# Moving the look for negative elements of adj from layer 0 to layer 3, and lists, ranks and descriptions ahead of layer 0's last additions

## The chip, the core and the metric

The kernel runs on one core of a Trainium2 chip. Its engines work side by side, each through its own queue in program order: TensorE (PE, with its weight loads PEld), VectorE (DVE), ScalarE (ACT), GpSimd (POOL) and SyncE (SP), which here only issues DMA transfers; ACT issues some too. The metric is the device time of one execution in microseconds.

## The reference

There is a table x of 2708 rows of 128 numbers and a weighted adjacency matrix adj of 2708 x 2708, of which some 0.6% and the diagonal are nonzero. Four layers each add a term to x, computed from h = max(layernorm(x), 0):

- Layer 0: x += (adj^T h) / column sums of adj.
- Layer 1: messages gelu(s_i + d_j + b) for every pair (i, j), weighted with adj[i, j] and summed over j; then an update with a gelu, a layernorm and a residual. s and d are h times two 128 x 128 matrices.
- Layer 2: agg = adj h, a matrix with a relu, and a GRU cell on it and h.
- Layer 3: graph attention with two heads, softmax over the neighbours (adj > 0, or the diagonal), a layernorm, a matrix and an elu for each head, and their mean.

## The kernel before

x, h and small tables stay in SBUF. Rows are taken in 22 tiles of 128 (the last has 20 rows), four tiles make a group (six groups, the last of two tiles), columns are taken in 22 blocks of 124.

**Layer 0** reads adj once, in cuts c = 0 to 5 of four column tiles, and in each cut the row groups s = 0 to 5. `load_cut` brings one piece of 512 rows x some 560 columns into a ring of four buffers `a` (DMA from SP); the pieces of the narrow cut 5 go to tiles `z` of their own. For each piece, `list_cut` finds on DVE the eight largest values of each row in each block of 124 columns with their positions (`val`, `col`), because layer 1 works on lists of the nonzero elements. `work_cut` turns the piece's blocks on PE (L409), copies them out of PSUM on ACT to `aT` (L413), stores them as adjT in DRAM (DMA from ACT, L363), and multiplies the piece into the sums (L384, PE). `look` (L395, ACT) passes over half a piece at a time with Relu(-a) and an accumulated sum in `below`; a sum above zero later makes the kernel take its dense path, since lists of the largest values don't hold negative elements. Small steps of the layernorms (`spread`, `sum_rows`, `sum_squares`, `normal_rows`) go between these on ACT.

The order of the work here is written out by hand: under `manual_schedule` every engine executes in the order of the program text. Cut 5's pieces are worked within cut 4; their lists are made later, in `list_last`.

**Hand-over.** After the last `work_cut` come `list_last(0)`, counts of row entries (`count_some`), `add(LAST)` (the last group's sums added to x, `invert` at L446), further lists, `rank(0)` (a matmul with a triangular matrix, L590, whose result goes to `ends` and, spread fourfold, to `ends4`, L591 and L592), the moments of x, lists 4 to 16, `add(LAST - 1)`. A second list of steps inside layer 1 then selects, describes and places the entries of the first tiles: `describe` splits the values of one tile into three bf16 parts with column numbers and ends (ACT, DVE, POOL); `select_rows` compares on DVE (L657) and shifts the result by one row with two DMAs from SP (`later`); `finish_rows` subtracts (L731); `fetch` multiplies on PE (L742); `place` picks each entry's value and column; `pass_on` spreads column numbers through DRAM; `columns` compares them.

**Layer 1** then runs in 22 periods, one tile each, with PE full. **Layer 2** reads adjT in chunks of 512 columns, and writes a byte `mask` of the nonzero elements. **Layer 3** goes through the row tiles in runs of 3, 8, 8 and 3: for each source tile and head, `weigh` makes weights on DVE (L1139) and PE multiplies them into sums (L1169). Between runs `evacuate` empties the PSUM banks by ACT and DVE (L1215), and `close` finishes two tiles at a time: moments on DVE, scaling on ACT (L136), turning on PE (L1243), a copy on ACT (`z4T`, L1246), matmuls (L1252), the elu on ACT, and the store of `y` (DMA from SP). These steps are generators that `follow` registers; `advance` takes the next step of each when a modelled clock, counted up by `spend`, has passed the units that the step yielded. At the end a `flag` with all reasons for the dense path is summed by a matmul and read by the engines.

Of the kernel before, what the change touches and what calls it, by code (L numbers as in the profile page):

```python
# [20 lines left out]
F32 = mybir.dt.float32  # L21
# [9 lines left out]
P = 128  # L31
# [29 lines left out]
def listed_layers(ctx: ExitStack, tc: tile.TileContext, x, adj, w, out, flag):  # L61
# [99 lines left out]
    below = keep.tile([P, 2 * len(GROUPS) ** 2], F32, name="below")  # L161
    nc.gpsimd.memset(below, 0.0)
# [129 lines left out]
    turned = l0.enter_context(tc.tile_pool(name="l0t", bufs=10))  # L292
# [72 lines left out]
    def work_cut(c, s, between=()):  # L365
# [23 lines left out]
        e0, e1 = t0 * P - lo, t0 * P - lo + span(t0, tk)[1]  # L389

        def look(half):
            q0, q1, m = (2 * half, 2 * half + 2, P) if gk == 4 else (half, half + 1, size(g0 + half))
            junk = pool.tile([P, 2, CH], U8, name="junk0", bufs=1)
            i = 2 * (len(GROUPS) * c + s) + half
            nc.scalar.activation(  # L395
                junk[0:m, 0 : q1 - q0, 0 : e1 - e0], a[0:m, q0:q1, e0:e1], AF.Relu, scale=-1.0,
                accum_out=below[0:m, i : i + 1],
            )

# [3 lines left out]
        for js in turns:  # L403
# [16 lines left out]
            turn_of = [t for t, v in enumerate(turns) if v is js][0]  # L420
            if len(turns) == 2 or turn_of % 2 == 1:
                look(turn_of * 2 // len(turns))
# [166 lines left out]
    def rank(t, p):  # L589
        nc.tensor.matmul(p[:, 0:NB], before, rows_n[:, t, :], start=True, stop=True)  # L590
        nc.vector.tensor_copy(ends[:, t, :], p[:, 0:NB])  # L591
        nc.vector.tensor_copy(ends4, p[:, 0:NB].unsqueeze(2).to_broadcast([P, NB, R]))  # L592
# [3 lines left out]
    add(LAST)  # L596
# [3 lines left out]
    rank(0, bank("p_r"))  # L600
    measure(LAST)
    for n in range(4, 17):
        list_last(n)
# [27 lines left out]
    with (  # L631
# [9 lines left out]
        def split(dst, src, rest):  # L641

            nc.scalar.copy(dst[0], src)
            nc.vector.tensor_tensor(rest, src, dst[0], ALU.subtract)
            nc.scalar.copy(dst[1], rest)
            nc.gpsimd.tensor_tensor(dst[2], rest, dst[1], ALU.subtract)

# [65 lines left out]
        def describe(t):  # L713
            x = xb[t % 2]
            rest = once.tile([P, NB, S], F32, name="v_r")
            split([x[:, :, q * S : (q + 1) * S] for q in range(3)], val[:, t, :, :], rest)
            nc.gpsimd.tensor_copy(x[:, :, 3 * S : 4 * S], col[:, t, :, :])
            nc.gpsimd.tensor_copy(x[:, :, C - 1], ends[:, t, :])
# [1204 lines left out]
```

## Time and profile before

| | |
|---|---|
| median of 3 runs | 1057.58 us (1057.03, 1057.58, 1063.91) |
| profiled execution, time | 1063.71 us |
| profiled execution, span | 1061.9 us |
| granted clock of PE, mean | 0.943 |
| PE busy | 934.5 us (88%) |
| PE weight loads busy | 817.3 us (77%) |
| DVE busy | 797.8 us (75%) |
| ACT busy | 518.4 us (49%) |
| POOL busy | 471.1 us (44%) |

In the trace's time the layers lie about so: layer 0 from 0 to 231 us, the hand-over to 287, layer 1 to 610, layer 2 to 777, layer 3 to the end. A row of a group has the line, the engine and operation, the tiles written and read with their shapes, how often, busy time and mean duration, and the engine's idle time just before with what ended it. A row of the timeline begins with the start and the duration in us; brackets hold the idle time before it and what ended that. A row of waits says who waited for whom: total us, times, longest. The share of an engine over the whole span is a mean of stages with different limits, so stretches of the span are read by themselves.

### The profile page before, as it was taken

The page shows a single profiled execution, that of the slowest core. Times are in us where ns is not written, and L with a number is a line of the kernel's source. Part 1 is how long each engine was busy: PE and PEld are TensorE (multiplying, and loading weights), DVE is VectorE, ACT ScalarE, POOL GpSimd, SP SyncE. Part 2 cuts the span into 40 slices and gives each one's busy share as a digit, 9 for nine tenths or more (in the row PEclk, how much of TensorE's full clock was granted, in tenths as well). Part 3 has the DMA queues.
Part 4 walks back from the last instruction along what each step waited for, and adds up shares of the span by engine and source line. Part 5 has one row for each costly group of instructions (what it writes and reads, how often), then busy time and mean ns, then how long its engine had stood idle before and what let it go on. Part 6 is the DMA issues. An engine that isn't in the chain of part 4 may idle for free. (4 is left out here: it accounts for less than half of the span.)

```text
span 1061.9 us, 23359 instructions
## 1 busy us (share of the span) xinstructions
PE 934.5 (88%) x8632; PEld 817.3 (77%) x8632; DVE 797.8 (75%) x2754; ACT 518.4 (49%) x1471; POOL 471.1 (44%) x589
## 2 busy tenths in 40 slices
PE   6799788972499999999999969999979999989983
PEld 5699688751499999999899824444568899989982
DVE  7999797747677878887868264656578977997793
ACT  6887678752466666667666521433322200330142
POOL 6222222312597778898979173344311300250042
PEclk9999898975699999999999979999989999999996
DMA  9799799521234343233322065556410000000000
GB/s 299 244 316 363 231 362 358 187 68 58 79 125 125 99 125 121 96 105 113 101 95 83 12 223 186 199 188 221 129 35 21 12 4 1 2 16 6 1 15 15
DMA packets 77091, 133.65 MB, mean 126 GB/s; under 512 B 13980, under 2 KB 29456, under 8 KB 76966
## 3 DMA queue, kind: packets, MB, share of 16 engines
q1 hardware_dynamic: 56986, 99.92, 29.0%
q10 hardware_dynamic: 19980, 32.14, 8.4%
q8 instruction: 70, 1.15, 0.5%
q14 instruction: 55, 0.45, 0.1%
HBM read 85.41 MB, written 30.87 MB: 109 GB/s over the span
## 5 line engine op out<-in xcount | busy, mean ns | idle before, releaser
L787 POOL TENSOR_SCALAR put<-count,line,value 128x128 f32<-128x128 f32 x176 | 204.5, 1176 | 37.0 <-DVE value L776 36.9
L1169 PE MATMUL att<-hv,wt 128*128 128x129 f32 x1672 | 195.4, 277 | 8.8 <-DVE wt L1139 7.3
L1169 PEld LDWEIGHTS att<-hv,wt 128*128 128x128 f32 x1672 | 191.8, 194 | 11.8 <-DVE wt L1139 7.0
L869 PE MATMUL p_m<-s,sel 128*128 128x128 bf16 x1452 | 162.7, 221 | 6.0 <-ACT g L881 5.8
L873 PE MATMUL p_m<-d,cols 124*128 124x128 bf16 (+1 forms) x1452 | 163.0, 221 | 0.7 <-DVE cols L818 0.7
L1139 DVE SCALAR_TENSOR_TENSOR wt<-row,lift,mask 128x1024 f32<-128x1024 f32 (+1 forms) x132 | 138.0, 1075 | 24.6 <-PE att L1169 24.5
L120 POOL TENSOR_TENSOR n_r<-n_r,minus_half 128x4 f32<-128x4 f32 (+1 forms) x28 | 39.9, 1425 | 236.2 <-DVE n_r L119 232.3
L384 PE MATMUL sums<-h,a 128*128 128x129 f32 (+1 forms) x880 | 124.5, 291 | 1.5 <-ACT h L136 1.5
L894 PE MATMUL agg<-put,g 128*128 128x128 f32 (+1 forms) x968 | 122.5, 278 | 0.0
L1308 PE MATMUL p_agg<-a,hs 128*128 128x512 f32 (+2 forms) x264 | 111.2, 564 | 12.2 <-issue 6.2
L384 PEld LDWEIGHTS sums<-h,a 128*128 128x128 f32 (+1 forms) x880 | 115.1, 206 | 2.8 <-issue 2.3
L894 PEld LDWEIGHTS agg<-put,g 128*128 128x128 f32 x968 | 113.1, 192 | 0.0
L869 PEld LDWEIGHTS <-sel 128*128 128x128 bf16 x1452 | 104.3, 98 | 7.5 <-issue 7.0
L873 PEld LDWEIGHTS <-cols 124*128 124x128 bf16 (+1 forms) x1452 | 103.5, 98 | 1.0 <-DVE cols L818 1.0
L409 PE MATMUL p_T<-ident,a 128*128 128x128 f32 (+1 forms) x440 | 75.4, 292 | 29.4 <-ACT aT L413 23.0
L796 ACT ACTIVATE put<-mine,value 128x128 f32<-128x128 bf16 x308 | 100.6, 392 | 0.0
L881 ACT ACTIVATE g<-p_m 128x512 f32<-128x512 f32 x132 | 72.7, 552 | 54.9 <-PE agg L894 41.2
L1308 PEld LDWEIGHTS p_agg<-a,hs 128*128 128x128 f32 (+1 forms) x264 | 48.3, 197 | 61.5 <-issue 53.6
L357 DVE FIND_INDEX8 col<-val,a 128x8 uint16<-128x124 f32 x342 | 91.7, 279 | 0.0
L355 DVE MAX8 val<-a 128x8 f32<-128x124 f32 x342 | 79.2, 273 | 13.0 <-DMA a<-in_adj 13.0
L409 PEld LDWEIGHTS p_T<-ident,a 128*128 128x128 f32 (+1 forms) x440 | 54.4, 149 | 40.5 <-ACT aT L413 28.4
L413 ACT COPY aT<-p_T 128x512 f32<-128x512 f32 (+2 forms) x122 | 67.9, 560 | 17.8 <-PE p_T L409 17.3
(271 smaller groups left out, 1563.4 us busy)
## 6 DMA issues: line engine op xcount, KB each, us to landing
adjT<-aT ACTq DMA_DIRECT2D x105, 256.0 KB
a<-adjT SPq DMA_DIRECT2D x20, 1280.0 KB
spread<-passed SPq DMA_DIRECT2D x22, 704.0 KB
later<-sel SPq DMA_DIRECT2D x22, 616.0 KB
a<-in_adj SPq DMA_DIRECT2D x5, 1152.0 KB
a<-in_adj SPq DMA_DIRECT2D x5, 1120.0 KB
a<-in_adj SPq DMA_DIRECT2D x5, 1088.0 KB
a<-in_adj SPq DMA_DIRECT2D x5, 1056.0 KB
```

The costliest lines, as they stand in the source:

```text
L355: nc.vector.max(val[0:m, n, b, :], v)
L357: nc.vector.max_index(col[0:m, n, b, :], val[0:m, n, b, :], v)
L384: nc.tensor.matmul(accs[c][q // 2][0:k, q % 2, :], a[0:m, n - g0, e : e + k], h0[0:m, n, :], start=(n == 0 and q % 2 == 0), stop=(n == NT ...
L409: nc.tensor.transpose(p[0:k, i * iw + q * P : i * iw + q * P + m], a[0:m, q, e : e + k], ident[0:m, 0:m])
L787: nc.gpsimd.tensor_scalar(st["put", 0][:, b, :], count, st["line"][:, b : b + 1], st["value"][:, b : b + 1], ALU.is_equal, ALU.mult,)
L796: nc.scalar.activation(st["put", 1][:, b - HP, :], st["mine"][:, b - HP, :], AF.Identity, scale=st["value"][:, b : b + 1])
L869: nc.tensor.matmul(p[:, b - b0, :], st["sel"][:, b, :], s3[:, q, t % 2, :], start=(q == 0), stop=False)
L873: nc.tensor.matmul(p[:, b - b0, :], st["cols"][0:kb, b, :], d3[0:kb, b, q, :], start=False, stop=(q == 2))
L894: nc.tensor.matmul(agg, g[:, b - 4 * k, :], put, start=(b == 0), stop=False)
L1139: nc.vector.scalar_tensor_tensor(wt[:, 0:n], row[:, k, c : c + n], lift[:, j, k : k + 1], mask[:, j, c : c + n], op0=ALU.max, op1=ALU.mult,)
L1169: nc.tensor.matmul(banks[s // 3][:, s % 3, :], wt[:, q * P : (q + 1) * P], hv[:, j, k, :], start=(v < 2 and s // 3 not in touched), stop=( ...
L1308: nc.tensor.matmul(pa[:, 0:n], h[0:k, j, :], a[0:k, j - j0, 0:n], start=(j == 0), stop=(j == NT - 1))
```

## The change

The look is taken out of `work_cut`, with its counters (`below`, 72 columns) and the three operations that added them to the flag at the end of layer 1. In layer 3 a new generator `look_through` reads adj again, in 44 half rows of tiles (128 rows x 1354 columns, 0.69 MB), alternately into the two halves of h's space, which layer 3 doesn't use. Each half is fetched by SP when the look before last has ended, and passed over by ACT in place with the same Relu(-a) and accumulated sum; one look every 4.2 units of the modelled clock, beginning with run 1. At its end three small DVE operations add the result to the flag.

In the hand-over, lists 1 to 16, the ranks of tiles 0, 1 and 2 and the descriptions of tiles 0 and 1 come ahead of `add(LAST)`; the fourfold spread of `ends` becomes a step of its own (`spread_ends`) that reads `ends` from SBUF; `describe` and `split` move out of layer 1's block; the step list at layer 1's start is put in another order. The pool of turned blocks gets 11 buffers instead of 10.

```diff
--- before.py
+++ after.py
@@ -158,8 +158,6 @@
     own = keep.tile([P, NT], F32, name="own")
     nc.gpsimd.memset(own, 0.0)
     inv = keep.tile([P, NT], F32, name="inv_deg")
-    below = keep.tile([P, 2 * len(GROUPS) ** 2], F32, name="below")
-    nc.gpsimd.memset(below, 0.0)
 
     HB = NB // 2
     HP = 8
@@ -289,7 +287,7 @@
     once0 = l0.enter_context(tc.tile_pool(name="l0h", bufs=1))
     pool = l0.enter_context(tc.tile_pool(name="l0k", bufs=2))
     marked = l0.enter_context(tc.tile_pool(name="l0n", bufs=8))
-    turned = l0.enter_context(tc.tile_pool(name="l0t", bufs=10))
+    turned = l0.enter_context(tc.tile_pool(name="l0t", bufs=11))
     sump = l0.enter_context(tc.tile_pool(name="l0p", bufs=4, space=PSUM))
     turnp = l0.enter_context(tc.tile_pool(name="l0q", bufs=2, space=PSUM))
     h0 = once0.tile([P, NT, D + 1], F32, name="h0")
@@ -385,17 +383,6 @@
                     accs[c][q // 2][0:k, q % 2, :], a[0:m, n - g0, e : e + k], h0[0:m, n, :],
                     start=(n == 0 and q % 2 == 0), stop=(n == NT - 1), skip_group_check=True,
                 )
-
-        e0, e1 = t0 * P - lo, t0 * P - lo + span(t0, tk)[1]
-
-        def look(half):
-            q0, q1, m = (2 * half, 2 * half + 2, P) if gk == 4 else (half, half + 1, size(g0 + half))
-            junk = pool.tile([P, 2, CH], U8, name="junk0", bufs=1)
-            i = 2 * (len(GROUPS) * c + s) + half
-            nc.scalar.activation(
-                junk[0:m, 0 : q1 - q0, 0 : e1 - e0], a[0:m, q0:q1, e0:e1], AF.Relu, scale=-1.0,
-                accum_out=below[0:m, i : i + 1],
-            )
 
         todo = list(range(g0, g0 + gk))
         js = list(range(t0, t0 + tk))
@@ -417,9 +404,6 @@
             ))
             for _ in range(2 if c == 0 else 1):
                 next(steps, None)
-            turn_of = [t for t, v in enumerate(turns) if v is js][0]
-            if len(turns) == 2 or turn_of % 2 == 1:
-                look(turn_of * 2 // len(turns))
             if c > 0 and todo and gk == 4:
                 products(todo.pop(0))
         for _ in steps:
@@ -589,18 +573,40 @@
     def rank(t, p):
         nc.tensor.matmul(p[:, 0:NB], before, rows_n[:, t, :], start=True, stop=True)
         nc.vector.tensor_copy(ends[:, t, :], p[:, 0:NB])
-        nc.vector.tensor_copy(ends4, p[:, 0:NB].unsqueeze(2).to_broadcast([P, NB, R]))
+
+    def spread_ends(t):
+        nc.vector.tensor_copy(ends4, ends[:, t, :].unsqueeze(2).to_broadcast([P, NB, R]))
+
+    def split(dst, src, rest):
+
+        nc.scalar.copy(dst[0], src)
+        nc.vector.tensor_tensor(rest, src, dst[0], ALU.subtract)
+        nc.scalar.copy(dst[1], rest)
+        nc.gpsimd.tensor_tensor(dst[2], rest, dst[1], ALU.subtract)
+
+    def describe(t, rest):
+        x = xb[t % 2]
+        split([x[:, :, q * S : (q + 1) * S] for q in range(3)], val[:, t, :, :], rest)
+        nc.gpsimd.tensor_copy(x[:, :, 3 * S : 4 * S], col[:, t, :, :])
+        nc.gpsimd.tensor_copy(x[:, :, C - 1], ends[:, t, :])
 
     list_last(0)
     count_some(0, 1)
-    add(LAST)
     for n in range(1, 4):
         list_last(n)
     count_some(1, 3)
-    rank(0, bank("p_r"))
+    for t in range(3):
+        rank(t, bank("p_r"))
+    for n in range(4, 14):
+        list_last(n)
+    for t in range(2):
+        describe(t, d_rest[:, 2 * t : 2 * t + 2, :].rearrange("p q d -> p (q d)")[:, 0 : NB * S].rearrange(
+            "p (b s) -> p b s", s=S
+        ))
+    for n in range(14, 17):
+        list_last(n)
+    add(LAST)
     measure(LAST)
-    for n in range(4, 17):
-        list_last(n)
     add(LAST - 1)
     destinations(LAST - 2)
     l0.close()
@@ -638,13 +644,6 @@
         tc.tile_pool(name="l1p", bufs=1, space=PSUM, reuse_waits="tile") as acc,
         tc.tile_pool(name="l1r", bufs=1, space=PSUM, reuse_waits="tile") as rpool,
     ):
-        def split(dst, src, rest):
-
-            nc.scalar.copy(dst[0], src)
-            nc.vector.tensor_tensor(rest, src, dst[0], ALU.subtract)
-            nc.scalar.copy(dst[1], rest)
-            nc.gpsimd.tensor_tensor(dst[2], rest, dst[1], ALU.subtract)
-
         def count_rows(t):
             some = work.tile([P, NB, S], BF16, name="some")
             nc.vector.tensor_scalar(some, val[:, t, :, :], 0.0, None, ALU.is_gt)
@@ -710,12 +709,8 @@
                         dst[0:TAIL, NT - 1, b : b + k, :], src[i * TAIL : (i + 1) * TAIL, 0:k, :]
                     )
 
-        def describe(t):
-            x = xb[t % 2]
-            rest = once.tile([P, NB, S], F32, name="v_r")
-            split([x[:, :, q * S : (q + 1) * S] for q in range(3)], val[:, t, :, :], rest)
-            nc.gpsimd.tensor_copy(x[:, :, 3 * S : 4 * S], col[:, t, :, :])
-            nc.gpsimd.tensor_copy(x[:, :, C - 1], ends[:, t, :])
+        def describe_next(t):
+            describe(t, once.tile([P, NB, S], F32, name="v_r"))
 
         def select_rows(t):
 
@@ -983,6 +978,7 @@
                     pass_on(t + 1)
                 if k == 1 and a:
                     rank(t + 3, rpool.tile([P, CH], F32, tag="r", name="p_r"))
+                    spread_ends(t + 3)
                 if k == 1 and last:
                     gather(t - 1, GB - 2)
                 elif k in (3, 5) and now:
@@ -1003,7 +999,7 @@
                 if k in (1, 2) and b:
                     fetch(t + 2, k - 1)
                 if k == 1 and a:
-                    describe(t + 3)
+                    describe_next(t + 3)
                 if k == 2:
                     if now and t % 2 == 0 and t + 2 < NT:
                         sources(t // 2 + 1)
@@ -1040,20 +1036,17 @@
             for k in range(1, GB):
                 put_more(t, k)
 
-        def rank_next(t):
-            rank(t, rpool.tile([P, CH], F32, tag="r", name="p_r"))
-
         def close_lists(_):
             ending.close()
 
         puts = ExitStack()
         for step, n in (
-            (select_rows, 0), (describe, 0), (rows, 5), (measure, 4), (turn_rows, 5), (split_destinations, 3),
-            (finish_rows, 0), (rows, 4), (fetch_both, 0), (turn_rows, 4), (rank_next, 1), (place, 0),
-            (destinations, 4), (pass_on, 0), (select_rows, 1), (describe, 1), (split_destinations, 4),
-            (destinations, 5), (sources, 0), (finish_rows, 1), (fetch_both, 1), (columns, 0), (rank_next, 2),
-            (split_destinations, 5), (place, 1), (pass_on, 1), (select_rows, 2), (describe, 2),
-            *((list_last, n) for n in range(17, NT)),
+            (spread_ends, 0), (select_rows, 0), (rows, 5), (measure, 4), (turn_rows, 5), (list_last, 17),
+            (finish_rows, 0), (fetch_both, 0), (spread_ends, 1), (select_rows, 1), (rows, 4),
+            (split_destinations, 3), (turn_rows, 4), (place, 0), (destinations, 4), (pass_on, 0), (list_last, 18),
+            (finish_rows, 1), (fetch_both, 1), (split_destinations, 4), (destinations, 5), (spread_ends, 2),
+            (select_rows, 2), (sources, 0), (describe_next, 2), (columns, 0), (place, 1), (split_destinations, 5),
+            (pass_on, 1), *((list_last, n) for n in range(19, NT)),
             (close_lists, 0),
         ):
             step(n)
@@ -1079,9 +1072,6 @@
         nc.vector.tensor_scalar(many, val[:, :, :, S - 1], 0.0, None, ALU.is_gt)
         nc.vector.reduce_sum(over[:, 1:2], many, AX.XY)
         nc.vector.tensor_tensor(flag, over[:, 0:1], over[:, 1:2], ALU.add)
-        nc.vector.tensor_scalar(below, below, 0.0, None, ALU.is_gt)
-        nc.vector.reduce_sum(over[:, 0:1], below, AX.X)
-        nc.vector.tensor_tensor(flag, flag, over[:, 0:1], ALU.add)
     lists.close()
 
 
@@ -1092,6 +1082,8 @@
     l3 = ctx.enter_context(tc.tile_pool(name="l3", bufs=1))
     h3 = l3.tile([P, NT, D], F32, name="h3")
     mask = l3.tile([P, NT, N], U8, name="mask")
+    below = l3.tile([P, 2 * NT + 1], F32, name="below")
+    nc.gpsimd.memset(below, 0.0)
     hv = l3.tile([P, NT, 2, D + 1], F32, name="hv")
     lift = l3.tile([P, NT, 2], F32, name="lift")
     row = l3.tile([P, 2, N], F32, name="row")
@@ -1274,6 +1266,29 @@
             m, i = size(t0 + q), (t0 + q) * P
             nc.sync.dma_start(out[i : i + m, :], y[0:m, q, :])
 
+    def look_through():
+
+        half = N // 2
+        seen = h.rearrange("p t d -> p (t d)")[:, 0:N].rearrange("p (q e) -> p q e", q=2)
+
+        def fetch_half(i):
+            n, q = divmod(i, 2)
+            m = size(n)
+            nc.sync.dma_start(seen[0:m, q, :], adj[n * P : n * P + m, q * half : (q + 1) * half])
+
+        for i in range(2):
+            fetch_half(i)
+        for i in range(2 * NT):
+            yield 4.2
+            v = seen[0 : size(i // 2), i % 2, :]
+            nc.scalar.activation(v, v, AF.Relu, scale=-1.0, accum_out=below[0 : size(i // 2), i : i + 1])
+            if i + 2 < 2 * NT:
+                fetch_half(i + 2)
+        yield 4
+        nc.vector.tensor_scalar(below, below, 0.0, None, ALU.is_gt)
+        nc.vector.reduce_sum(below[:, 2 * NT : 2 * NT + 1], below[:, 0 : 2 * NT], AX.X)
+        nc.vector.tensor_tensor(flag, flag, below[:, 2 * NT : 2 * NT + 1], ALU.add)
+
     def close_run(run, sums, apart=9):
 
         for first in range(0, run[1], 2):
@@ -1447,6 +1462,7 @@
         nc.gpsimd.memset(padded[q], 0.0)
 
     with tc.tile_pool(name="l3w", bufs=5) as wpool, tc.manual_schedule():
+        follow(look_through())
         for run, numbers in zip(RUNS[1:], ((2, 3, 4, 5, 0, 1), (2, 3, 4, 5, 0, 1), (2, 3))):
 
             def work_off(last=last, banks=banks):
```

## The prediction

> **What bounds the kernel now.** I read the busy time by stage first: the stages have different limits, and the chain that ended last holds only the final 1.2 us. Columns: stretch in us, its length, busy us (instructions) of PE, weight load, DVE, ACT, POOL, the granted clock, DMA share, GB/s.
>
> ```profile
> 8.00:168.00 160.00, 135.57 (x1059) 126.67 (x1059) 145.30 (x963) 128.85 (x361) 46.40 (x134) 0.97 0.92 310
> 168.00:231.00 63.00, 62.62 (x433) 52.23 (x433) 38.36 (x248) 48.07 (x136) 15.84 (x47) 0.88 0.59 206
> 231.00:287.00 56.00, 16.19 (x146) 13.14 (x146) 43.31 (x172) 18.06 (x54) 17.49 (x25) 0.59 0.21 65
> 287.00:610.00 323.00, 313.22 (x4458) 307.55 (x4455) 240.65 (x585) 210.05 (x636) 252.92 (x251) 0.99 0.31 98
> 777.00:1062.00 285.00, 251.97 (x2106) 243.12 (x2106) 224.27 (x481) 60.06 (x143) 58.55 (x59) 0.95 0.04 11
> ```
>
> Row 1 is layer 0's first four cuts: DVE, PE, ACT and the DMA engines are all nearly full, a ring of four that hold each other. Row 2 is the cut where the last strips are worked off: PE alone, 62.6 of 63 us. Row 3 is the hand-over to layer 1: DVE, with 12.7 us of holes. In rows 4 and 5 PE is full; ACT is busy only 60 of 285 us in row 5.
>
> Then the looks, by line over layer 0 (count | busy us, mean ns | idle before):
>
> ```profile
> L395 ACT ACTIVATE junk<-a 128x1024 uint8<-128x1024 f32 (+2 forms) x60 | 59.1, 985 | 5.0 <-DMA a<-in_adj 2.7 <-ACT aT L413 1.2 <-DMA z<-in_adj 0.9
> L395 ACT ACTIVATION_READ_ACCUMULATOR junk<-a 128x1 f32 (+1 forms) x60 | 11.8, 196 | 0.0
> L395 ACT ACTIVATE junk<-z 128x296 uint8<-128x296 f32 (+2 forms) x12 | 5.2, 432 | 2.6 <-DMA a<-in_adj 2.6
> L395 ACT ACTIVATION_READ_ACCUMULATOR junk<-z 128x1 f32 (+1 forms) x12 | 2.3, 192 | 0.0
> ```
>
> They are 59.1+11.8+5.2+2.3 = 78.4 us of ACT. Who waits in layer 0 (total us, times, longest), PE's row first, then DVE's:
>
> ```profile
> PE p_T L409 <- ACT aT L413: 23.3, 23, 3.1
> DVE inv_deg L446 <- ACT sums L563: 18.0, 1, 18.0
> DVE val L355 <- DMA a<-in_adj: 13.0, 6, 6.2
> DVE inv_deg L446 <- PE sums L384: 4.4, 2, 3.7
> ```
>
> PE waits for ACT's copy of the turned blocks; DVE waits for loads, which wait until all readers, the look among them, have left a ring buffer. The 18 us is DVE standing in front of the last additions. The timeline of the hand-over:
>
> ```profile
> 230.64 0.20 PE L590 MATMUL p_r<-rows_n,before 128*128 128x22 bf16 x1
> 256.89 0.18 DVE L591 CAST ends<-p_r 128x22 bf16<-128x22 f32 x1 [2.29 <-PE p_r L590]
> 269.43 1.62 DVE L731 TENSOR_TENSOR sel<-sel,later 128x2816 bf16<-128x2816 bf16 x1 [3.51 <-DMA later<-sel]
> 284.61 1.62 DVE L731 TENSOR_TENSOR sel<-sel,later 128x2816 bf16<-128x2816 bf16 x1 [2.89 <-DMA later<-sel]
> 286.29 0.53 PE L742 MATMUL y<-xb,sel 128*128 128x37 bf16 x11 [6.18 <-DVE sel L731]
> ```
>
> PE reaches the first rank at 230.64, when its layer 0 ends, and runs without holes from 286.29, when tile 2 is selected. Last, one closing of layer 3:
>
> ```profile
> 944.08 1.65 ACT L136 ACTIVATE att_s<-att_s,n_r 128x128 f32<-128x128 f32 x4 [4.24 <-DVE n_r L130]
> 944.62 1.48 PE L1243 MATMUL p_aT<-ident,att_s 128*128 128x128 f32 x4 [1.06 <-ACT att_s L136]
> 946.15 0.78 ACT L1246 ACTIVATE z4T<-p_aT,b,g 128x512 f32<-128x512 f32 x1 [0.42 <-PE p_aT L1243]
> ```
>
> ACT is idle on the whole there, but a full PE waits on it at such points.
>
> **What the skill says.** "ScalarE: Activation LUTs", section "What ACT_TABLE_LOAD costs": an ACTIVATE with immediates takes 186 ns + 0.833 N. The trace agrees: 1039 ns by it for N = 1024, about 1054 shown. "Perfetto Trace Analysis", "Optimization Strategy": interleaving stages with different full engines may pay; rows 1 and 5 are such a pair for ACT. "DMA: Bandwidth & Descriptors", "Issuing engines are not separate DMA queues": all transfers share 16 engines. The trace fits: the write-backs (ACT) and loads (SP) together make the 0.92 of row 1.
>
> **Looks out of layer 0.** Per ring step (four blocks by four), ACT loses two looks of 1.05+0.19 = 2.5 us. In cut 0 the ACT copies come every 8.25 us (PE waits at 21.3, 29.5, 37.8, 46.2), while DVE lists a step in about 7.1 and PE needs about 5.5. Without looks ACT needs 5.75, and DVE paces. Two gains follow. First, PE's lag: DVE begins to list cut 4 at 164.25, PE to turn it at 172.33, 8.1 later; with no wait for ACT it should follow within 2: **6 us**. Second, DVE's own waits for loads before cut 4 are 2.27 (55.3), 1.59 (120.2), 6.17 (133.6), 2.60 (164.3) = 12.6 us. The first and last are late releases and should go. The middle two stand behind SP: it issues a load at 111.78, then the late weights until 125.1, then the next at 125.69, landed by 133.6. The load at 111.78 waited for the reads of cut 2's third group, whose listing ended at 105.0; the looks and the diagonal reads behind them on ACT came later. That chain can start 4 to 8 us earlier, its 14 us stay. I take 8 of the 12.6. From cut 4 on PE is full: 172.33 to 230.70 = 58.4 us, which the looks don't touch, so both gains arrive whole: **14 us**. Ends: the DVE floor is 145.3 us for row 1's 160, plus the lag, about 20; if the DMA engines (0.92 busy) hold the ring, 5. One buffer more for turned blocks has no wait of weight; nothing either way.
>
> **Lists, ranks, descriptions.** In DVE's order the last additions stood behind one list; the change puts lists 1 to 16, three ranks and two descriptions before them. But rank 0 waits for PE's matmul, which stands behind all of layer 0's products. So DVE does lists 0 to 3 and counts (about 5 us) and then stands again until PE is done: the 18 us wait stays under another name, as before. Behind DVE there wait lists 4 to 16, then the additions, then ACT and POOL for the rows of group 5. From PE's end: three ends 0.6, ten lists at 0.85 = 8.5, two descriptions 0.7 and 1 of wait (ACT's copies alternate with DVE), three lists 2.6, additions 1.1 and 1.7 with the moments 1.0 between, the spread ends 0.24, the first comparison 1.6: first selection done at 19.3 (before: 246.45-230.64 = 15.8). From there ranks and descriptions for tiles 1 and 2 no longer interrupt, and other work stands between each shifted copy (4.7 to 6.8 us from the end of the comparison to its use) and its subtraction: factors, moments, list 17, placing, split. I sum row by row to the third subtraction's end at 51 to 53; before 286.15-230.64 = 55.5. Removed are the DVE holes 0.72, 2.29, 1.22, 0.47, 3.51, 2.89 = 11.1; added 1.1 of additions formerly done earlier, and about 6 of new waits. **3 us gained**, from -1 to 5. POOL's and SP's queues are passed by the two descriptions (about 1.2 us of POOL each) and the earlier shifted copies: POOL has 38 us of holes there. Removing the three operations on the old counters (under 1 us of DVE, amid holes) and adding the new ones costs nothing; without that cover, 0.6.
>
> **Looks in layer 3.** 44 half rows: (186 + 0.833 x 1354 = 1.31) + 0.19 = 1.5 us by the page (the 1024 and 296 rows give 1.33), 66 us of ACT in holes of 225. 29.3 MB more are loaded at a DMA share of 0.04. SP issues each half only after the look before last; the output stores on SP wait behind. Looks come every 4.2 units of a clock that sets 0.29 for a matmul pair measuring 0.277, so about 4.0 us apart, done in runs 1 and 2 (218 units against 189). In the six closings of runs 0 and 1 a look falls between ACT's scaling and its copy of the turned rows; ACT idles there only 0.4, 1.5, 1.6, 0.8, 0.4, 0.4 us, so PE's next matmuls wait 1.1+0+0+0.7+1.1+1.1 = 4, less a little slack: **3 us lost**, from 0 (ACT runs ahead) to 6. The copies that free PE's banks between runs follow 42 us or more of idle ACT; nothing.
>
> **Sum.** -14 -3 +3 = -14. On the profiled execution (span 1061.9, time 1063.7) that gives 1049.7; that execution is 6.1 above the median of the runs, 1057.6, so I predict **1044**.
>
> **Rivals.** (a) *The ring is held by DMA.* For: 0.92 busy; loads take 8 to 10 us from issue. Against: stretches of 10 us moved 390 GB/s, the mean is 310. Layer 0 gains 3 to 5, the rest cancels: **1054**. (b) *Layer 3's look holds ACT's queue*, slower. A half's fetch starts when the look before last ends, so two looks cost one landing plus 1.5 us; 8.0 are allowed. From a landing of 6.5 us on ACT falls behind, and the closings and bank copies queue behind waiting looks. At 8 us each look costs 4.85 instead of 4.0: 44 x 0.85 = 37 us lost, 17 gained: **1078**. For: layer 0's loads took 8 to 10. Against: these were 1.1 MB amid writes; 1.28 MB took under 6.1 us at layer 2's start (issued 608.22, used 614.33), and this is 0.69 MB on idle engines. (c) *Everything in layer 0 yields* and ACT runs ahead: -20 -4 +1: **1035**.
>
> **Chances.** Forecast 0.60, (a) 0.20, (b) 0.09, (c) 0.11. The range 1034 to 1058 takes in (a) and most of (c) and the bounds of both unknown costs; it leaves (b) out. A measurement of this kernel tells about 1% from no change (1047 and 1068 are the marks): faster 0.62 (the forecast's better part and c), same 0.29, slower 0.09.
>
> **What would show it.** PE's first rank near 216 instead of 230.6; PE's waits for turned copies under 8 us; cut 4's turning within 3 us of DVE; DVE again idle about 15 us, now ahead of the rank's ends; third subtraction 51 to 53 us after the rank; layer 3 longer by 3 with PE waiting in closings. Wrong if the ring's loads still land late, or if ACT waits for adj's halves while PE waits for ACT.

## The result, and the profile after

The changed kernel takes 1052.3 us in the median of its runs (1050.9 to 1056.1), the kernel before, beside it, 1060.8: a ratio of 0.9926 [0.9906, 0.9947]. So it is faster by 8.5 us, 0.7%, where 13.6 were forecast. Of the 8 us by which the forecast of 1044 misses, 3 are its starting point (1057.6 was the median of three runs, 1060.8 is that of ten), and 5 are sizes that were wrong. The profiled execution took 1052.42 us, span 1050.6; against the profiled execution before (1063.71) that is 11.3 less. Both single traces can be compared stage by stage, but their difference is some 3 us larger than that of the medians, because the one before lay 2.9 above its median.

The busy time by stage, in the stretches shown for the kernel before (us from and to, length, busy us and instructions of PE, weight load, DVE, ACT, POOL, granted clock, DMA share, GB/s):

```profile
8.00:168.00 160.00, 139.74 (x1099) 131.83 (x1100) 147.41 (x980) 90.52 (x278) 48.66 (x141) 0.95 0.95 320
168.00:231.00 63.00, 52.27 (x403) 42.92 (x402) 43.79 (x289) 28.21 (x78) 13.62 (x40) 0.94 0.49 180
231.00:287.00 56.00, 23.74 (x249) 20.29 (x250) 41.25 (x126) 24.51 (x75) 25.81 (x33) 0.62 0.24 78
287.00:610.00 323.00, 310.01 (x4352) 301.12 (x4352) 238.08 (x600) 204.74 (x617) 249.38 (x248) 0.98 0.33 107
777.00:1050.00 273.00, 243.29 (x2057) 234.86 (x2056) 219.65 (x468) 118.43 (x226) 57.12 (x58) 0.96 0.36 113
```

ACT is relieved where it was meant to be: 90.5 busy us in row 1 (128.9 before), 28.2 in row 2 (48.1). It is loaded in row 5 (118.4, from 60.1). The DMA share of row 1 has risen to 0.95. The same stages as marks, in us, taken from the first and last instructions of each:

| | before | after | difference |
|---|---|---|---|
| DVE begins to list cut 4 | 164.25 | 156.01 | -8.2 |
| from there until PE begins to turn cut 4 (the lag) | 8.1 | 9.5 | +1.5 |
| from there to PE's first rank (cut 4 on PE) | 58.3 | 55.5 | -2.8 |
| **first rank: end of layer 0** | 230.64 | 221.03 | **-9.6** |
| third subtraction, behind the first rank | 55.6 | 52.1 | -3.5 |
| **first tile of layer 1 closed, behind the first rank** | 71.1 | 71.8 | **+0.7** |
| rest of layer 1 | 305.0 | 304.0 | -1.0 |
| to the first matmul of layer 3's run 1 | 217.8 | 218.0 | +0.3 |
| **from there to the end (looks included)** | 237.4 | 235.7 | **-1.7** |

Nearly all of the gain is in layer 0; from the first closed tile on, the differences are of the size by which single traces of like code differ. The waits of layer 0 in the changed kernel (who waited, for whom: us, times, longest), lines from the list of waits up to 231 us:

```profile
PE p_T L396 <- ACT aT L400: 22.0, 16, 3.6
DVE ends L575 <- PE p_r L574: 18.7, 2, 18.5
ACT aT L400 <- DMA a<-in_adj: 7.9, 3, 4.9
DVE inv_deg L430 <- PE sums L382: 5.8, 2, 5.5
DVE val L353 <- DMA a<-in_adj: 5.4, 3, 4.9
```

DVE waits 5.4 us for loads (13.0 before), almost all in one wait of 4.88 at 127.89, behind the late weights. DVE's 18 us ahead of the hand-over stand under the rank's ends, as the forecast said they would. But **PE's waits for the copies of turned blocks are 22.0 us, and were 23.3**, though ACT has 58 us less to do in these two stages. And there is a row that isn't in the list of the kernel before: ACT's copy of a turned block, which reads only what PE has written, is held by a *load*.

The hand-over and its first period, in order of time:

```profile
221.03 0.21 PE L574 MATMUL p_r<-rows_n,before 128*128 128x22 bf16 x2
221.25 0.27 DVE L575 CAST ends<-p_r 128x22 bf16<-128x22 f32 x2 [18.55 <-PE p_r L574]
...
244.71 1.63 DVE L726 TENSOR_TENSOR sel<-sel,later 128x2816 bf16<-128x2816 bf16 x1 [1.15 <-DMA later<-sel]
...
271.53 1.59 DVE L726 TENSOR_TENSOR sel<-sel,later 128x2816 bf16<-128x2816 bf16 x1
...
273.18 0.44 PE L737 MATMUL y<-xb,sel 128*128 128x37 bf16 x11
...
274.77 0.33 PE L864 MATMUL p_m<-s,sel 128*128 128x128 bf16 x3 [1.14 <-ACT g L876]
...
278.50 0.17 ACT L742 COPY line<-y 128x8 f32<-128x8 f32 x1 [3.21 <-POOL put L782]
...
280.88 0.33 PE L864 MATMUL p_m<-s,sel 128*128 128x128 bf16 x3 [1.12 <-ACT g L876]
...
284.57 0.48 PE L864 MATMUL p_m<-s,sel 128*128 128x128 bf16 x3 [2.18 <-ACT g L876]
```

The third subtraction no longer waits for the shifted copy (2.89 us before), and the fetch for tile 2 starts 52.2 us behind the rank. Then a wait opens that the kernel before hasn't in this stretch: ACT stands 3.21 us at its copy of the line for tile 2 until POOL has made puts of tile 0, and behind it in ACT's queue stand the g's that PE wants.

Layer 3, a closing of run 0 with two looks (L1284) in it, PE's turning, ACT and the matmuls that follow:

```profile
825.83 1.65 ACT L136 ACTIVATE att_s<-att_s,n_r 128x128 f32<-128x128 f32 x4 [10.00 <-DVE n_r L130]
...
826.47 1.39 PE L1235 MATMUL p_aT<-ident,att_s 128*128 128x128 f32 x4 [0.58 <-ACT att_s L136]
...
827.38 1.31 ACT L1284 ACTIVATE hs<-hs 128x1354 f32<-128x1354 f32 x1
...
827.70 1.95 PE L1161 MATMUL att<-hv,wt 128*128 128x129 f32 x16
...
828.61 0.19 ACT L1284 ACTIVATION_READ_ACCUMULATOR hs<-hs 128x1 f32 x1
828.70 0.76 ACT L1238 ACTIVATE z4T<-p_aT,b,g 128x512 f32<-128x512 f32 x1
829.36 1.32 ACT L1284 ACTIVATE hs<-hs 128x1354 f32<-128x1354 f32 x1
...
829.51 1.16 PE L1244 MATMUL p_o<-ff1T,z4T 128*128 128x128 f32 x8
```

A look does fall between ACT's scaling and its copy z4T, and takes the 1.3 us that the page "ScalarE: Activation LUTs" of the Trainium skill prices it at (section "What ACT_TABLE_LOAD costs": 186 ns + 0.833 N gives 1314 ns for N = 1354; the 44 looks had a median of 1332), with 0.19 for its sum. But the matmuls p_o carry no wait, because PE had other matmuls in its queue, those of 827.70, until z4T was done.

### The profile page after: what moved, and what is told of

It is laid out like the page before. It is cut to its first block, busy times and chain, and to the rows that moved or that the text cites. A ratio compares the mean times of both kernels' runs of the same rounds, so it can differ in the third digit from the quotient of the medians.

```text
span 1050.6 us, 23379 instructions
## 1 busy us (share of the span) xinstructions
PE 926.0 (88%) x8632; PEld 810.5 (77%) x8632; DVE 795.5 (76%) x2754; ACT 519.6 (49%) x1415; POOL 471.7 (45%) x589
## 5 line engine op out<-in xcount | busy, mean ns | idle before, releaser
L1131 DVE SCALAR_TENSOR_TENSOR wt<-row,lift,mask 128x1024 f32<-128x1024 f32 (+1 forms) x132 | 138.8, 1083 | 23.3 <-PE att L1161 23.2
L382 PE MATMUL sums<-h,a 128*128 128x129 f32 (+1 forms) x880 | 120.3, 285 | 0.4 <-ACT h L136 0.4
L864 PEld LDWEIGHTS <-sel 128*128 128x128 bf16 x1452 | 103.6, 98 | 12.2 <-issue 11.7
L382 PEld LDWEIGHTS sums<-h,a 128*128 128x128 f32 (+1 forms) x880 | 111.6, 200 | 1.6 <-POOL near L336 0.8
L1323 PEld LDWEIGHTS p_agg<-a,hs 128*128 128x128 f32 (+1 forms) x264 | 48.1, 195 | 63.4 <-issue 60.3
```

The lines of the kernel that those rows point to most:

```text
L382: nc.tensor.matmul(accs[c][q // 2][0:k, q % 2, :], a[0:m, n - g0, e : e + k], h0[0:m, n, :], start=(n == 0 and q % 2 == 0), stop=(n == NT ...
L864: nc.tensor.matmul(p[:, b - b0, :], st["sel"][:, b, :], s3[:, q, t % 2, :], start=(q == 0), stop=False)
L1131: nc.vector.scalar_tensor_tensor(wt[:, 0:n], row[:, k, c : c + n], lift[:, j, k : k + 1], mask[:, j, c : c + n], op0=ALU.max, op1=ALU.mult,)
L1323: nc.tensor.matmul(pa[:, 0:n], h[0:k, j, :], a[0:k, j - j0, 0:n], start=(j == 0), stop=(j == NT - 1))
```

## The experiments

The first four runs were measured together, with runs of the kernel before among them; so were the next four, and so the last four, these on another chip. Within such a set times are compared directly, across sets only the ratios to the kernel before, and even these with care. Marks such as the first rank come from one trace of each kernel.

**Layer 3's look left out.** The changed kernel, with nothing else touched:

```diff
-        follow(look_through())
```

> The changed kernel without the looks in layer 3 (negative elements are then looked for nowhere). If the looks of layer 3 cost nothing, as the stage marks of the two traces suggest (run 1 to the end: 237.4 us before, 235.7 after), the time is the changed kernel's within 1 us: 0.992 to 0.993 of the kernel before. If they cost the 3 us of the prediction, it is 3 us under that, about 0.990.

Measured: 1051.62 us, ratio 0.9912 [0.9891, 0.9934] beside 0.9926 with the looks. From run 1 of layer 3 to the end its trace needs 236.3 us, with the looks 235.7. Over all fourteen traces this stretch takes 235.5 to 235.8 us in the ten kernels with these looks and 234.9 to 237.4 in the four without. So 66 us of looks on ACT and 29 MB of loads cost nothing that can be seen, at most about 1 us by the traces. The times alone would not settle it: by their intervals a cost of up to some 5 us is possible.

**Looks left out of the kernel before**, the old order of the hand-over kept:

```diff
-            turn_of = [t for t, v in enumerate(turns) if v is js][0]
-            if len(turns) == 2 or turn_of % 2 == 1:
-                look(turn_of * 2 // len(turns))
...
-        nc.vector.tensor_scalar(below, below, 0.0, None, ALU.is_gt)
-        nc.vector.reduce_sum(over[:, 0:1], below, AX.X)
-        nc.vector.tensor_tensor(flag, flag, over[:, 0:1], ALU.add)
```

> The kernel before without the looks of layer 0, nothing else changed (negative elements are looked for nowhere). If layer 0 alone makes the gain, PE's first rank comes at about 221 instead of 230.6 us and the time is 8 to 10 us under the kernel before, about 0.992, no worse than the changed kernel. If the new order of the hand-over brings 3 us of the gain, as the prediction has it, this kernel stays 3 us behind the changed one without layer 3's looks.

Measured: 1053.69 us, ratio 0.9935 [0.9913, 0.9957]. DVE begins cut 4 at 157.65 (164.25 with the looks), PE follows 7.5 us later, and the first rank comes at 224.63, not near 221: cut 4 takes 59.4 us here and 55.5 in the changed kernel, at a granted clock of 0.94 against 1.00 (see PE's granted clock below). By the ratios this part alone makes 0.65% of the 0.74% that the changed kernel gains, about half of the 14 us that the forecast gave it. (The medians beside it, 1053.7 and 1058.5, give only 0.46%.) The changed kernel without layer 3's looks, the run above, lies 2.1 us lower; the two ranges overlap (1049.1 to 1055.0 and 1052.2 to 1055.8), and this kernel also has 10 turned blocks where that one has 11, so the 3 us of the new order are neither shown nor excluded by this pair.

**New order only.** Looks kept in layer 0, the lists, ranks and descriptions in the changed kernel's order:

```diff
-    add(LAST)
...
-    rank(0, bank("p_r"))
+    for t in range(3):
+        rank(t, bank("p_r"))
+    for n in range(4, 14):
+        list_last(n)
+    for t in range(2):
+        describe(t, ...)
+    for n in range(14, 17):
+        list_last(n)
+    add(LAST)
```

> The kernel before, looks in layer 0 kept, with the new order of the hand-over alone. If POOL's placing of the first values sets the end of the hand-over, the first tile's sums are closed 71 to 72 us after the first rank as before (301.75-230.64 = 71.1), and the time is that of the kernel before within 1 us (0.999 to 1.001). By the prediction's step it is 3 us shorter, 0.997.

Measured: 1062.09 us over 20 runs, ratio 1.0028 [1.0006, 1.0049]. Its third subtraction ends 52.1 us behind the first rank, as forecast, and its first tile closes 71.9 us behind it: no earlier than in the kernel before (71.1) or in that without looks (71.8). The time is 0.3% longer, with looks left in layer 0. So the reorder gains nothing here.

**Lists before ranks.** All lists and the last additions ahead of the three ranks, the descriptions behind them; this fills the 18 us in which DVE waits for the rank:

```diff
+    for n in range(4, 17):
+        list_last(n)
+    add(LAST)
+    measure(LAST)
     for t in range(3):
         rank(t, bank("p_r"))
-    for n in range(4, 14):
-        list_last(n)
     for t in range(2):
         describe(t, ...)
-    for n in range(14, 17):
-        list_last(n)
-    add(LAST)
-    measure(LAST)
```

> The changed kernel with lists 4 to 16, the last additions and the moments ahead of the three ranks on DVE, so that they fall into the 18.5 us in which DVE stands before the first rank. If DVE's order sets the hand-over, 11 to 13 us of DVE work leave it: the third subtraction ends about 40 us after the first rank instead of 52, and the time is 8 to 11 us under the changed kernel, about 0.983 of the kernel before. If POOL's placing holds the end, less: 0 to 4 us under the changed kernel.

Measured: 1043.53 us, ratio 0.9844 [0.9816, 0.9873]. From its list of waits up to 231 us and its timeline:

```profile
DVE ends L575 <- PE p_r L574: 1.9, 2, 1.8
```

```profile
222.21 0.21 PE L574 MATMUL p_r<-rows_n,before 128*128 128x22 bf16 x2
222.43 0.27 DVE L575 CAST ends<-p_r 128x22 bf16<-128x22 f32 x2 [1.76 <-PE p_r L574]
...
259.66 1.59 DVE L724 TENSOR_TENSOR sel<-sel,later 128x2816 bf16<-128x2816 bf16 x1
```

DVE's wait at the rank has shrunk from 18.7 to 1.9 us, the third subtraction ends 39.0 us behind the rank (52.1) and the first tile closes 58.5 behind it (71.8). So DVE's list of work lies on the road from the rank to the first tile: 13 us taken off the list shorten the road by 13 us. In the changed kernel ten lists, three more and the additions still lay on it.

The next four kernels stand on this one. **Three buffers for the line** that ACT copies and POOL's puts read:

```diff
-                st["line"] = work.tile([P, HP], F32, name="line")
+                st["line"] = three.tile([P, HP], F32, name="line")
```

> The kernel with the lists before the ranks, with three buffers instead of two for the small tile line that ACT copies for POOL. If ACT's 3.2 us wait for POOL's first eight values, which holds the activations that PE waits for, is what is late next, the first tile closes 3 us earlier after the first rank (55.5 instead of 58.5) and the time falls by 2 to 4 us. If POOL's 16 values themselves hold the next periods, nothing moves by more than 1 us.

**Late weights later**, loaded behind the last piece of cut 4 in place of the middle of cut 2:

```diff
-            W_msgT, W_ihT, W_hhT = load(late, "W_msgT"), ...
...
+    W_msgT, W_ihT, W_hhT = load(late, "W_msgT"), ...
```

> The kernel with the lists before the ranks; SP loads the late weights after cut 4's last piece instead of in the middle of cut 2. If these twelve transfers hold up cut 3 (SP busy with them from 107 to 120 us, DVE waits 4.9 us for the next load, PE 3.6 for ACT), DVE's wait there goes and PE begins to turn cut 4 4 to 6 us earlier (160 instead of 165.5), the time falls by 3 to 6 us. If the 16 DMA engines are full in cut 3 anyway, the waits only move, and it is within 1.5 us.

**Two turned blocks to a store**, of 512 KB; 72 stores in layer 0 in place of 122:

```diff
-    turned = l0.enter_context(tc.tile_pool(name="l0t", bufs=11))
+    turned = l0.enter_context(tc.tile_pool(name="l0t", bufs=5))
...
-            aT = turned.tile([P, CH], F32, name="aT")
-            nc.scalar.copy(aT[0:k, 0 : n * iw], p[0:k, 0 : n * iw])
+                second = (js[0] - t0) % 2
+                if not second:
+                    pair = turned.tile([P, 2, CH], F32, name="aT")
+                nc.scalar.copy(pair[0:k, second, 0:iw], p[0:k, 0:iw])
...
+                if second:
+                    written.append((adjT[0:k, js[0] - 1 : js[0] + 1, i0 : i0 + iw], pair[0:k, :, 0:iw]))
```

> The kernel with the lists before the ranks; two turned blocks leave by one store of 512 KB where there were two of 256 KB. Every transfer takes one of eight completion semaphores in turn, and in the trace ACT's stores start within 0.1 us of the landing of the transfer that had their semaphore before (144.54 to 144.61). If this turn of eight is what holds ACT, half as many stores take most of PE's 21 us of waits for turned copies away, and layer 0's products end 4 to 7 us earlier. If the DMA engines' rate is what holds both, the loads land no earlier, and it is within 2 us.

**All three together**, the three edits above in one kernel:

> The last three edits together on the kernel with the lists before the ranks. If each is worth what its first reading says, 8 to 14 us less than that kernel; if the DMA rate and POOL's values hold the two places, 0 to 3 us.

Measured, with the marks of their traces (us; lag and cut as in the table of the result):

| | median | ratio | DVE at cut 4 | lag | cut 4 on PE | first rank | first tile closed behind it |
|---|---|---|---|---|---|---|---|
| lists before ranks | 1043.53 | 0.9844 [0.9816, 0.9873] | 156.6 | 8.0 | 57.6 | 222.2 | 58.5 |
| + three line buffers | 1037.17 | 0.9775 [0.9741, 0.9808] | 155.2 | 9.3 | 55.4 | 220.0 | 53.9 |
| + weights later | 1035.52 | 0.9760 [0.9727, 0.9793] | 150.9 | 5.3 | 57.5 | 213.6 | 58.6 |
| + paired stores | 1035.45 | 0.9754 [0.9722, 0.9785] | 155.8 | 2.9 | 56.0 | 214.7 | 58.9 |
| + all three | 1029.04 | 0.9687 [0.9655, 0.9719] | 151.7 | 2.6 | 60.5 | 214.8 | 54.0 |

Each acts where it was meant to. Later weights let DVE reach cut 4 five us earlier; paired stores bring PE's lag down to 2.9 us, with ACT's work on the blocks unchanged (68.3 us). What was expected of the paired stores came true in part only: the first rank is 7.5 us earlier, but PE's waits for turned copies, of which most was to go, are still 18.3 us (21.4 without pairing). In these traces the two don't add: together the lag is hardly smaller, PE takes longer for cut 4, and the first rank comes at 214.8 (PE's clock has a part in that, see below). All three together beat both kernels, by 3.1% and 2.4%.

Then the same single edits on the changed kernel itself, and the lists-first kernel once more, on one chip.

> The changed kernel itself, with nothing but two turned blocks in one 512 KB store (five pairs of blocks in the pool in place of eleven blocks). Theory (the lag that stayed is ACT held at issuing its stores, which share their completion semaphores with the loads): PE begins to turn cut 4 within 4 us of DVE's beginning to list it (9.5 in the changed kernel), first rank near 214.8 in place of 221.0, the time 6 us under the changed kernel, some 1046. Rival (PE's lag is its own work, and pairing helps only with the other order of the hand-over): lag stays above 8, time within 2 us of the changed kernel.

> The changed kernel itself, with the late weights loaded behind the last piece of cut 4 in place of in the middle of cut 2. Theory: DVE's load wait of 4.9 us near 123 goes, DVE begins cut 4 near 151 in place of 156, PE's lag there is near 5, first rank near 213.7, the time 7 us under the changed kernel, some 1045. Rival (a cover is missing elsewhere: the weights then delay layer 1's first tiles): first rank early, but the first tile closes over 74 us behind it and the time is within 2 us of the changed kernel.

> Kernel of the run with lists before ranks once more, beside the other three on one chip, to have the differences without a change of chip: 1044, first tile closed 58.5 us behind the first rank. If it comes near 1038, the gain of 7 to 9 us that three line buffers, later weights and paired stores showed over it was mostly the chip's.

> The changed kernel itself, with three buffers for the line that POOL reads, in place of two. Theory (the hand-over's 3.5 us are given back because ACT's copy of the line for tile 2 waits for POOL's puts of tile 0, and PE then waits for g): that wait of 3.2 us and PE's waits for g (1.1, 1.1 and 2.2) are gone, the first tile closes near 68 behind the first rank in place of 71.8, time 3 to 4 us under the changed kernel, some 1048. Rival (POOL's puts themselves end last): the first tile closes 71 to 72 behind the first rank and the time is within 1.5 us of the changed kernel.

| | median | ratio | DVE at cut 4 | lag | cut 4 on PE | first rank | first tile closed behind it |
|---|---|---|---|---|---|---|---|
| changed kernel (measured apart) | 1052.30 | 0.9926 [0.9906, 0.9947] | 156.0 | 9.5 | 55.5 | 221.0 | 71.8 |
| + paired stores | 1051.13 | 0.9920 [0.9897, 0.9942] | 157.4 | 3.3 | 57.5 | 218.2 | 71.8 |
| + weights later | 1048.93 | 0.9892 [0.9841, 0.9942] | 151.8 | 5.8 | 57.7 | 215.2 | 71.9 |
| + three line buffers | 1051.50 | 0.9911 [0.9883, 0.9940] | 157.2 | 6.3 | 57.4 | 220.9 | 67.0 |
| lists first again | 1044.84 | 0.9868 [0.9813, 0.9923] | 156.1 | 9.5 | 55.3 | 220.9 | 58.6 |

*Lists first again* came out at 1044.8, not near 1038: so its own gain stands on a second chip. Nor was the set of the single edits a fast one (the kernel before took 1061.9 us there, 1058.5 and 1060.0 in the other two), so the 6 to 8 us by which they lie under it aren't the set's. From its trace to theirs the spans fall by 7.3 to 7.6 us, of which the first rank and the first tile explain 5.6 (three line buffers), 7.3 (weights) and 5.9 (paired stores).

*Paired stores* on the changed kernel: the lag fell from 9.5 to 3.3 us, as the theory has it. The first rank, expected at 214.8, came only at 218.2, and the time is within 2 us of the changed kernel, as the rival said. PE's waits for turned copies sum to 20.1 us, hardly less than with the lag (22.0). DVE waits for one load as in the changed kernel (5.8 us at 129.6, there 4.9 at 127.9), and in cut 4 there remains, from the list of waits of 160 to 181 us (all engines):

```profile
ACT aT L410 <- DMA z<-in_adj: 3.7, 1, 3.7
PEld p_T L396 <- ACT aT L410: 2.8, 1, 2.8
...
PE p_T L396 <- ACT aT L410: 2.6, 1, 2.6
```

The chain is still there: a load, now of a piece `z`, holds a store at its issue, the store holds ACT's copies, and they hold PE.

*Weights later*: DVE at cut 4 and the lag are where the theory put them (151.8, 5.8), the rank 1.5 us later than expected, the time 1048.9 for 1045. The rival's delay in layer 1 isn't there: the first tile closes 71.9 behind the rank.

*Three line buffers*: the first tile closes 67.0 behind the rank, expected 68, but the time, expected at 1048, is 1051.5. From the lists of waits of 231 to 290 us, first of the changed kernel:

```profile
PE p_m L864 <- ACT g L876: 4.4, 3, 2.2
ACT line L742 <- POOL put L782: 3.2, 1, 3.2
```

and then of the same kernel with three line buffers, where ACT's wait is gone from the list:

```profile
PE p_m L864 <- ACT g L876: 1.3, 2, 1.1
```

So this wait is what took the hand-over's gain. Of the 4.8 us that it frees 1.5 are given back at once, in the second tile (14.9 us from the first closing in place of 13.4). At the end of the kernel no gain can be told from the changed kernel's own spread.

## Why the prediction was wrong

**Layer 0: -14 forecast, -9.6 in the traces.** The forecast had two terms. *DVE's waits for loads, 8 of 12.6 us*: right. DVE begins cut 4 8.2 us earlier, and the first and last of its waits are gone. *PE's lag, 8.1 to 2, worth 6*: **this is the step that failed.** The lag came to 9.5, and in six traces with this layer 0 (the changed kernel and the five runs that leave its layer 0 alone) to 6.3 to 9.5, in none to 2. From DVE's beginning to the first rank 65.0 us pass (63.7 to 65.6 in the six), 66.4 before and 60.4 by the forecast.

The step took PE's waits for turned copies for waits for ACT's work, to end "with no wait for ACT" when the looks went. Of the kernel before that was true: in 22.0 of the 23.3 us ACT was at work. With the looks gone PE's waits stay at 22.0 us, for two reasons. In 14.7 us of them ACT still works, mostly on the copies and on steps of the layernorms; ten of the sixteen waits, 9.3 us in all, lie before 47 us. In the other 7.3 us ACT is idle. What holds it there is seen at 132 to 146 us of the changed kernel's timeline:

```profile
132.37 0.37 SPq L313 DMA_DIRECT2D a<-in_adj  x1
...
139.08 0.60 ACT L400 COPY aT<-p_T 128x512 f32<-128x512 f32 x1
...
144.61 0.33 ACTq L361 DMA_DIRECT2D adjT<-aT  x1
...
145.25 0.58 ACT L400 COPY aT<-p_T 128x512 f32<-128x512 f32 x1
...
145.88 1.11 PE L396 MATMUL p_T<-ident,a 128*128 128x128 f32 x4 [3.46 <-ACT aT L400]
```

After its copy at 139.08 ACT's queue stands until 144.61, at the issue of a store. The semaphore events of the trace say why (a semaphore is a counter by which a transfer tells that it has landed). The transfers issued by SP and by ACT report their end on eight semaphores between them, and an issue waits until the transfer before it on its semaphore has landed (rows of both queues on two of the eight, us):

```
issued   by   what            semaphore  landed
121.98   SP   load a          103        132.29
132.37   SP   load a          103        144.54
144.61   ACT  store adjT      103        149.44
125.07   SP   load a          105        137.13
137.21   ACT  store adjT      105        142.82
```

The store at 144.61 waits for a load that has nothing to do with it and takes 12.2 us to land, and PE loses 3.46 us to that, in a stage with a mean DMA share of 0.95. Added up over layer 0 (stretches of over 0.2 us), ACT stands idle ahead of issues of stores until such a landing for 27.6 us, and for 13.8 before the change. With paired stores these are 12.2, 15.7 and 13.3 us in the three kernels that have them, and the lag is 2.9, 3.3 and 2.6, while the copies take 68.3 us with and without. So the lag hung on the stores and not on the copies. Whether it is the number of turns at the semaphores or the larger transfers that helps, these runs don't separate. The sum of PE's waits, which the forecast went by, is no measure of the lag: it is 18.3, 20.1 and 15.7 us in the same three.

**PE's granted clock** is a term that neither the forecast nor the marks take in. Cut 4, from PE's beginning to the first rank, in the kernel before, the changed kernel, and the changed kernel with paired stores; then the stretch of the changed kernel in which PE waits for the store shown above (columns as before):

```profile
172.33:230.64 58.31, 57.93 (x414) 48.17 (x414) 38.06 (x245) 45.26 (x129) 13.59 (x40) 0.91 0.55 193
165.55:221.03 55.48, 53.29 (x414) 44.30 (x413) 36.87 (x239) 30.04 (x81) 13.62 (x40) 1.00 0.61 222
160.70:218.21 57.51, 54.94 (x413) 45.99 (x413) 37.26 (x243) 30.19 (x81) 13.56 (x40) 0.97 0.62 225
144.50:151.40 6.90, 5.52 (x26) 5.52 (x27) 6.90 (x45) 3.60 (x10) 1.27 (x1) 0.51 0.96 307
```

In the five traces in which the clock was 1.00 all through cut 4, the cut took 55.3 to 56.0 us; in the others (0.91 to 0.97) 57.4 to 60.5. So the -2.8 of cut 4, which the forecast held fixed at 58.4, goes with the clock, and so do the 2 us that cut 4 is longer with paired stores on the changed kernel and part of the 4.5 that it is longer with all three edits than with paired stores alone. The lag goes with it too: in the seven traces with single stores, the late weights in their old place and no looks in layer 0, it is 9.3 to 9.5 where the clock was halved for 6.8 us around 144 to 151, 7.5 and 8.0 where it was for 3.4, and 6.3 in the one where it wasn't. In the changed kernel's layer 0 each of the four halved stretches begins in a wait of PE or up to 0.5 us behind one. So about half of what pairing takes from the lag may be the clock's: none of the three kernels with paired stores has a halved stretch there. No run sets the clock apart from the waits, so what brings such a stretch on is open; five waits of 2.0 to 2.7 us in cut 4 were followed by none.

Whether both terms would arrive whole, as the forecast said, stays open as well. On the changed kernel pairing took 6.3 us from the lag and 2.8 from the first rank; on the lists-first kernel, with the same layer 0, 5.1 and 7.5. The same layer 0 puts the first rank anywhere from 220.0 to 222.2 us in the six traces above, and at 214.7 and 218.2 in these two.

**Hand-over: -3 forecast, +0.7 in the traces**, which is no difference: with the old order and without looks the first tile closes 71.8 us behind the rank too. The sum of rows was right at its mark: the third subtraction 52.1 us behind the rank, forecast 51 to 53; DVE idle 18.5 ahead of the rank's ends, forecast about 15. (Its items up to the first selection add up to 19.0, not 19.3; nothing hangs on that.) The term failed in equating that mark with the time when PE runs without holes. PE's first closing needs the line and the g's from ACT, and with the selection earlier, ACT comes to the line's two buffers before POOL has left them: 19.7 us from the fetch for tile 2 to the first closing, 15.5 before, 14.8 with three buffers. The wait that took the place of the one removed was not among the rivals.

**Layer 3: +3 forecast, 0 measured.** The looks fall into the closings as forecast and cost what was priced. The error was to charge PE with ACT's delay at 827 to 829: over the layer PE waits 9.4 us in all for att_s (10.5 before) and 0.2 for z4T (0.2 before). The forecast set a look's length against ACT's idle time ahead of z4T; what counts is how long PE's own queue keeps it busy behind z4T. In the six closings of the kernel before, p_o began 0.8 to 1.6 us after z4T was done, and the looks delayed z4T by 0 to 0.8 us: in the closing shown, 0.05 us of that slack is left. So the term was wrong, and narrowly so. As -3 and +3 had cancelled in the forecast's sum, these two errors do too; that is luck.

**Rivals.** Of (a), the ring held by DMA, the mechanism had a large part, through ACT's stores rather than through loads alone, but its 3 to 5 us in layer 0 were too few. Its 1054 lay nearer to the measured 1052.3 than the forecast's 1044 by the starting point only: counted from 1060.8, it would be 1057 and the forecast 1047. (b) didn't occur: adj's halves made ACT wait 37.6 us in 27 waits of at most 2.6, in time it had to spare. (At 8 us to a landing its two looks make 9.5 us, 4.75 each and not 4.85, so it should have read about 1074.) (c) would have needed PE close behind DVE.

**Open.** In the fourteen single traces the 21 tiles of layer 1 behind the first take 303.9 to 307.6 us, though hardly anything in them differs. The two longest, one of them that of paired stores on the changed kernel, hold 5 us at half clock; the others, with 0 to 3.4 us of it, still spread from 303.9 to 307.0. So where early gains of 3 to 5 us stay is not settled, and why single edits showed more on the lists-first kernel than on the changed one isn't either. The eleventh turned block, which the forecast put at nothing, was not tried alone.

## What to carry to other kernels

A wait for an engine's result doesn't say that the engine is busy: look at what stands ahead of that result in its queue, issues of transfers included, before taking work off it. Compare stages of two traces only with the granted clock of each beside them: here 2 to 3 us of a cut of 55 went with it. When a stage is moved earlier, follow it on to the next thing that the full engine waits for, since a buffer count that was ample may become the wait. An engine that stands idle ahead of a join should be given the work that stands behind the join: 18 us of DVE's idle time, filled with lists and additions, were worth as much as the whole change.

## What had not been expected of the hardware

In the changed kernel ACT, which issues its own stores, was held up to 4.9 us by another queue's loads, through completion semaphores that both queues take in turn. The wait is an instruction of its own ahead of the store's issue (at 144.56, on semaphore 103), so it belongs to how the program was built; that the chip asks for it isn't shown. PE's granted clock fell to a half in stretches of 3.4 us or more, in the changed kernel's layer 0 always in or just behind a wait of PE. And 44 looks of 1.5 us each with 29 MB of loads beside a full PE cost nothing to be measured: 235.5 to 235.8 us from run 1 of layer 3 to the end with them, 234.9 to 237.4 without.
